# Layer 2's low-rank adapters folded into eight projection matrices while layer 1's experts run, with a reordered head and a pinned preparation of layer 3

## The chip, the cores and the metric

The kernel runs on one core of a Trainium2 chip. The metric is the device time of one execution in microseconds. TensorE (PE) does the matmuls and its weight loads are listed as PEld; VectorE is DVE, ScalarE is ACT, GpSimd is POOL, and SyncE (SP) issues most DMAs. Indirect DMAs (gathers by a list of indices) are issued by POOL. Everything is fp32.

## The reference, cut to what matters

Four layers run over a residual stream `x` of 32 sequences by 64 tokens by 512 values. Each layer is a conditioning step that depends on the sequence, followed by a feed-forward or attention block, and its result is added to `x`. Layer 0 is attention and seven experts, layer 1 is 32 experts with four chosen per token, layer 2 is a soft mixture of 16 experts, layer 3 is attention over a paged cache and a small product. The conditioning of layer 2 is what the change rewrites:

```python
def _L2_cond_ref(x, W, A, Bm, scalings, adapter_idx):
    N_ADAPTERS, RANK = (8, 16)
    H = jnp.einsum('btd,od->bto', x, W)
    A_b = A[adapter_idx]
    B_b = Bm[adapter_idx]
    s_b = scalings[adapter_idx]
    xa = jnp.einsum('btd,brd->btr', x, A_b)
    delta = jnp.einsum('btr,bor->bto', xa, B_b)
    delta = jax.lax.stop_gradient(delta * s_b[:, None, None])
    return H + delta
...
x = x + _L2_ffn_ref(_L2_cond_ref(x, L2_cond_W, ..., itok_B_0_6), ...)
```

So every sequence has one of eight adapters of rank 16, and its 64 tokens are multiplied by `W` transposed plus a low-rank product.

## The kernel before, in words

The 2048 rows of `x` are 16 tiles of 128 rows, and a tile holds two sequences. A matmul of the program is two instructions in the trace, since the values are fp32. A scheduler orders the instructions when the kernel is built; `g.pin` and `held` keep an operation in program order on its engine, `g.first` does so for the first matmul of a group, and a load marked `later` keeps its place.

The head (0 to about 366 us) loads constants, `x` and layer 0's weights on SP's queue in program order, gathers each sequence's 64x64 conditioning matrix (`wsel`) on POOL by an index `i_cond` that DVE computes from the conditions, and begins with the matmuls `mix`. Layer 0's experts follow to about 572 us. Beside them, once for each output tile, a generator called a `Side` puts in a piece of other work: `layer3_ahead` (line 2342) prepares index tables for layer 3's cache. Its operations on DVE are not pinned.

Layer 1 routes to about 690 us, and its experts run to about 1091 us. Their weights `wt` are gathered on POOL; the matmuls are `gu` (L1351), transposes `tp` (L1330) and `y` (L1364); DVE adds the bias `bd` into `yo`, four buffers, and SP writes it to the table `ys`. The `Side` here is `layer2_ahead` (line 1872), which loads layer 2's constants, makes a mask of adapters, and computes norms of layer 2's `mu` from 16 row blocks (`mus`).

Layer 2 takes about 1097 to 2045 us, 58.5 us a tile. For tile i it runs the soft mixture while it prepares tile i + 1: class `Lora` transposes the tile (`turn`, into `fT`), multiplies it with all eight adapters' A at once (`adapter`, L2110), masks the result by sequence on DVE (`am`, L2114), and multiplies with W and with B into one bank (`product`, L2122 and L2123). The layer normalisation after it goes over DVE (`st`, `ve`, `xl`), POOL (`rs`, gamma, beta, `nn`) and ACT. The residual of the tile after that comes from layer 1's table: `fetch` gathers four rows per token from `ys` (`yk`, three buffers) on POOL, and four pinned additions on DVE, add(0) to add(3), put them on `x`. The mixture's own order on TensorE in a tile is: dispatch (`ep`, `hp`), combine(0) to combine(3) (`gp`, L2311, one bank, emptied by DVE's `gT` copy, L2315) and project(0) to project(3) (`out`, L2320). POOL also gathers rows of layer 3's cache (`kvst`). In layer 2's start the load of `w2` (4 MB) goes out on ACT's queue.

Of the kernel before, what the change touches and what calls it, by code (L numbers as in the profile page):

```python
# [13 lines left out]
I32 = mybir.dt.int32  # L14
# [133 lines left out]
def _layout(i):  # L148
# [52 lines left out]
    a["w_2"] = _chunks(i["L2_cond_W"].T)  # L201
    a["w_a"] = _chunks(i["L2_cond_A"].reshape(P, D).T)
    a["w_b"] = i["L2_cond_Bm"].transpose(0, 2, 1).reshape(P, D)
# [49 lines left out]
class Prog:  # L253
# [96 lines left out]
    def per_half(self, pool, name):  # L350


        t = pool.tile([P, NT], I32, name=f"ih_{name}")
        for h in range(2):
            self.nc.sync.dma_start(
                out=t[64 * h : 64 * h + 64, :], in_=self.a[name][h].partition_broadcast(64)
            )
        f = pool.tile([P, NT], F32, name=f"fh_{name}")
        self.nc.vector.tensor_copy(f, t)
        return f  # L360

# [65 lines left out]
def layer0(g, w3, pool3):  # L427
    tc, nc, a = g.tc, g.nc, g.a
    with ExitStack() as ctx:
        keep = ctx.enter_context(tc.tile_pool(name="l0keep", bufs=1))  # L430
        g.constants(keep, "cst01")
        clear = g.results(keep)
        xs = g.stream("x0")
        ln2 = g.load(keep, "ln2")
        m = Moe(g, ctx, keep, E0, K0, [C0] * E0, V0, "w_e0", W0, l0_expert, ln2)
        with ExitStack() as c1:
            wp = c1.enter_context(tc.tile_pool(name="l0w", bufs=1))
            sb = c1.enter_context(tc.tile_pool(name="l0sb", bufs=2))
            at0 = g.cond_rows(wp, "cond0")
            x, other = {}, {}  # L440
# [12 lines left out]
            load(0)  # L453
            swapped(1)
            load(1)
            load(2)
            w = {k: g.load(wp, k) for k in ("ln1", "w_lat", "w_q", "w_kn", "w_kr", "w_v", "w_o", "w_r0")}
            shared = Shared(g)
# [524 lines left out]
def l1_expert(g, sb, hT, gate, up, bias, **kw):  # L983

    nc = g.nc
    ga = sb.tile([P, gate.shape[1]], F32, name="ga")
    nc.vector.tensor_scalar(ga, gate, bias[:, 0:1], 7.0, ALU.add, ALU.min)
    sg = sb.tile([P, gate.shape[1]], F32, name="sg", **kw)
    nc.scalar.activation(sg, ga, AF.Sigmoid, scale=1.702)  # L989
    up_ = sb.tile([P, gate.shape[1]], F32, name="up")  # L990
    nc.vector.tensor_scalar(up_, up, bias[:, 1:2], 7.0, ALU.add, ALU.min)
    nc.vector.tensor_scalar(up_, up_, -7.0, 1.0, ALU.max, ALU.add)
    g.pin(nc.gpsimd.tensor_tensor(ga, ga, sg, ALU.mult))  # L993
    nc.vector.tensor_tensor(hT, up_, ga, ALU.mult)


class Moe:
# [67 lines left out]
    def bias_of(self, e):  # L1065
        if self.bias and e < self.E and e not in self.bds:
            self.bds[e] = self.xp.tile([P, D], F32, name="bd", bufs=4)
            self.ask_bias(self.bds[e], e)
        return self.bds.get(e)
# [132 lines left out]
    def beyond(self):  # L1202
# [6 lines left out]
        with tc.If(n > 0), ExitStack() as ctx:  # L1209
# [67 lines left out]
            for t in range(V):  # L1277
                wt = sb.tile([P, self.wlen], F32, name="vwt", bufs=2)
                g.gather(wt, g.a[self.wname], widx[:, t : t + 1])
                xr = sb.tile([P, D], F32, name="vxr", bufs=1)  # L1280
                g.gather(xr, self.rows, stok[:, t : t + 1])
                xT = g.transpose4(ps, sb, xr, "vxT", self.scale)
                wg, wu, wd, bias = self.parts(wt)
                y = ffn(g, sb, ps, xT, wg, wu, wd, self.act, bias)
                yo = sb.tile([P, D], F32, name="vyo", bufs=2)
                if self.bias:
                    bd = sb.tile([P, D], F32, name="vbd", bufs=1)
                    g.gather(bd, g.a[self.bias], each[:, t : t + 1])
                    nc.vector.tensor_tensor(yo, y, bd, ALU.add)
                else:  # L1290
                    g.evac(yo, y)
                r = (self.tiles + t) * P
                nc.sync.dma_start(out=self.ys[r : r + P, :], in_=yo)
# [10 lines left out]
    def run(self, xs, per_tile):  # L1304
# [114 lines left out]
        def combined(pool, i, bufs):  # L1419
            x = g.load_x(pool, xs, i, bufs)  # L1420
            for k in range(K):
                kw = dict(name="yk", bufs=3) if k < 3 else dict(name="xl")
                yk = pool.tile([P, D], F32, **kw)
                g.gather(yk, self.ys, self.slot[:, i, k : k + 1], later=True)
                g.pin(nc.vector.scalar_tensor_tensor(x, yk, self.gates[:, i, k : k + 1], x, ALU.mult, ALU.add))
            return x

        def fetch(pool, i, bufs):
# [4 lines left out]
            def rows(k):  # L1433
                yk = pool.tile([P, D], F32, name="yk", bufs=3)
                g.gather(yk, self.ys, self.slot[:, i, k : k + 1], later=True)
                adds.append(partial(add, yk, k))
# [5 lines left out]

            for k in range(3):
                rows(k)
# [427 lines left out]
def layer2_ahead(g, w):  # L1872

    nc, a, first, pool = g.nc, g.a, w["first"], w["pool"]
    names = ("w_2", "w_a", "w_b", "mu", "w1")
    for k in names:
        w[k] = (pool if k in ("mu", "w1") else first).tile(list(a[k].shape), F32, name=f"sb_{k}", tag=f"sb_{k}")

    w["mask"] = pool.tile([P, B], F32, name="mask2")

    w["cmu"] = cmu = pool.tile([P, 16], F32, name="cmu")
    for k in names:
        for c in range(4 if k in ("mu", "w1") else 1):
            part = slice(None) if k not in ("mu", "w1") else (slice(None), slice(c, c + 1))
            g.dma(w[k][part], a[k][part])
            yield
    sb = w["sb"]
    scale = g.load_bcast(pool, "scale2")
    ad = g.load_bcast(pool, "adapt", I32)
    adf = pool.tile([P, B], F32, name="adf")  # L1890
    s8 = g.load(pool, "scal")
# [5 lines left out]
    nc.vector.tensor_copy(sc, sp)  # L1897
    nc.vector.tensor_scalar(w["mask"], adf, g.c("pd16"), sc, ALU.is_equal, ALU.mult)
    yield
    cs = pool.tile([P, 16], F32, name="cs2")  # L1900
    mus = {}
    for e in range(18):
# [6 lines left out]
        yield  # L1909
        if e < 16:  # L1910
            yield
    cn = g.power(pool, cs, "half", "cn")
    yield
    nc.vector.tensor_scalar(cn, cn, 1e-12, None, ALU.max)
    nc.vector.reciprocal(cmu, cn)
    nc.vector.tensor_scalar(cmu, cmu, scale, None, ALU.mult)


def layer2(g, w, combined, first, w3):
    tc, nc, a = g.tc, g.nc, g.a  # L1920
    with ExitStack() as ctx:
# [14 lines left out]
        x.append(t)  # L1936
        lora.adapter()
        yp = lora.product()
# [6 lines left out]
        next(norm)  # L1945
        lora.adapter()
        xn = next(norm)
# [11 lines left out]
        for i in range(NT + 1):  # L1959
# [31 lines left out]
            if early:  # L1991
                lora.turn()
                mix.sums()
                lora.adapter()
                soft.highest()
# [30 lines left out]
            if mix and not early:  # L2026
# [3 lines left out]
                mix.dispatch(0)  # L2030
                if lora:
                    lora.adapter()
                mix.turn(2)
                if lora:
                    norm = l2_norm_pieces(g, w, sb, s2, lora.product())
                    next(norm)
                    if i + 2 == NT:

                        w3["w_kv3"] = first.tile([P, 4, D], F32, name="w_kv3", tag="sb_w_2")
                        g.dma(w3["w_kv3"], a["w_kv3"])  # L2040
                        w3["x3"] = [first.tile([P, D], F32, name="x3", tag=f"sb_{k}") for k in ("w_a", "w_b")]
                        for j in range(2):
# [48 lines left out]
class Lora:  # L2091
# [12 lines left out]

    def adapter(self):

        g, nc, w, i = self.g, self.g.nc, self.w, self.i
        ap = self.ps.tile([P, 2, T], F32, name="ap2", tag="tp")
        for c in range(4):
            g.first(c, nc.tensor.matmul(  # L2110
                ap.rearrange("p b t -> p (b t)"), w["w_a"][:, c, :], self.xT[:, c, :], start=c == 0, stop=c == 3
            ))
        self.am = self.s2.tile([P, 2, T], F32, name="am")
        g.pin(nc.vector.tensor_tensor(  # L2114
            self.am, ap, w["mask"][:, 2 * i : 2 * i + 2].unsqueeze(2).to_broadcast([P, 2, T]), ALU.mult
        ))

    def product(self):
        g, nc, w = self.g, self.g.nc, self.w
        yp = self.ps.tile([P, D], F32, name="yp", tag="mm")  # L2120
        for c in range(4):
            g.first(c, nc.tensor.matmul(yp, self.xT[:, c, :], w["w_2"][:, c, :], start=c == 0, stop=False))  # L2122
        nc.tensor.matmul(yp, self.am.rearrange("p b t -> p (b t)"), w["w_b"], start=False, stop=True)  # L2123
        return yp

    def run(self):
        self.turn()
        self.adapter()
        return self.product()

# [211 lines left out]
def layer3_ahead(g, pool, w):  # L2342


    tc, nc, a = g.tc, g.nc, g.a
    w["kpos"] = pool.tile([P, B], F32, name="kpos")
# [7 lines left out]
    g.constants(sb, "cst3", later=True)  # L2354
    start = g.per_half(sb, "kvlen2")
    kvl = g.load_bcast(sb, "kvlen", I32)
# [5 lines left out]
    yield  # L2362

    w["ridx"] = ridx = sb.tile([P, NT], I32, name="ridx")
# [173 lines left out]
def layer3(g, w, xs, xb):  # L2538
# [3 lines left out]
    with ExitStack() as ctx:  # L2542
# [37 lines left out]
        with ExitStack() as c1:  # L2580
# [38 lines left out]
            for u in range(len(units) + 5):  # L2619
# [10 lines left out]
                if u < len(units):  # L2630
# [8 lines left out]
                    late = not z and i >= NT - LATE  # L2639
                    out = wp.tile([P, D], F32, name=f"qlate{i}") if late else sb.tile([P, D], F32, name="qkv3", bufs=6)  # L2640
                    outs.append(out)
# [310 lines left out]
```

## Time and profile before

| what | value |
| --- | --- |
| median of 3 runs | 2501.28 us (2495.75 to 2509.42) |
| profiled execution | 2500.39 us |
| its span | 2498.6 us |
| mean granted TensorE clock | 0.987 |
| PE busy | 2397.1 us, 96% |
| PEld busy | 1602.9 us, 64% |
| DVE busy | 1425.6 us, 57% |
| ACT busy | 716.1 us, 29% |
| POOL busy | 878.7 us, 35% |
| DMA moved | 341.46 MB, mean 137 GB/s |

The profiled execution is a single one, and the sums are made against its time. "Busy" counts an engine's instructions; several matmuls are in the pipeline at once, so a difference of start times is a better cost of a matmul than its duration. A row of a group names the line, the engine, the operation, the tile written and the tiles read, the shape, the count, then busy time in us and the mean ns of one, and last the idle time of the engine before these instructions and what ended it.

### The profile page before, as it was taken

To read this page: it belongs to the slowest core of one execution; us is meant where nothing else is said; L and a number is where in the kernel's file an instruction comes from. 1 tells how busy PE (TensorE), PEld (TensorE's weight loads), DVE (VectorE), ACT (ScalarE), POOL (GpSimd) and SP (SyncE) were. 2 spreads that over 40 slices of the span, in tenths; PEclk is the share of its full clock that TensorE was granted. 3 is DMA by queue.
4 is the path that set the end of the run, shared out by engine and by line. 5 is a ranking of instruction groups with operands and counts; after the bars stand their busy time and mean duration, and the time that the engine had idled before them with its cause. 6 is when DMAs were issued, how large, how long until landed. Compare 5 with 4: busy or idle time off the path is not lost.

```text
span 2498.6 us, 42594 instructions
## 1 busy us (share of the span) xinstructions
PE 2397.1 (96%) x16628; PEld 1602.9 (64%) x16643; DVE 1425.6 (57%) x3482; ACT 716.1 (29%) x1491; POOL 878.7 (35%) x923
## 2 busy tenths in 40 slices
PE   6999989999799999979999999999999999999998
PEld 4777766666566666747666666666666665446555
DVE  4667865835755545447445445554445441569887
ACT  2444521112311111102222222222222221246664
POOL 2122235604144434524333333333333221574440
PEclk9999999999799999989999999999999999999999
DMA  7242135537467977844222222222222223524441
GB/s 257 99 150 98 60 112 177 178 114 256 152 210 262 372 252 253 288 135 150 75 75 75 74 75 75 75 74 75 75 76 78 85 62 117 181 83 138 140 136 51
DMA packets 133560, 341.46 MB, mean 137 GB/s; under 512 B 24153, under 2 KB 25209, under 8 KB 126048
## 3 DMA queue, kind: packets, MB, share of 16 engines
q1 hardware_dynamic: 91184, 189.62, 22.0%
q0 software_dynamic: 41296, 142.68, 18.2%
q10 hardware_dynamic: 864, 6.29, 0.6%
q8 instruction: 135, 2.21, 0.4%
q14 instruction: 81, 0.66, 0.1%
HBM read 247.31 MB, written 107.22 MB: 142 GB/s over the span
## 4 chain that ended last, share of the span: by engine, by line
PE 50%; DVE 3%; issue 1%; POOL 1%; DMA 1%; ACT 1%; ACTq 0%; POOLq 0%; DVEq 0%
PE out L2320 9%; PE lp L2179 8%; PE zp L2256 8%; PE pp L2636 4%; PE hp L2288 3%; PE gp L2311 3%; PE yp L2122 2%; PE y L2887 2%; PE pT L2839 2%; PE sp L2817 2%; PE op L2865 2%; PE ep L2265 1%; PE kp L2790 1%; PE ap L2110 1%; PE out L2326 1%
## 5 line engine op out<-in xcount | busy, mean ns | idle before, releaser
L1351 PE MATMUL gu<-xT,wt 128*128 128x320 f32 (+5 forms) x1536 | 397.4, 406 | 6.6 <-DVE xT L1338 6.1
L1351 PEld LDWEIGHTS gu<-xT,wt 128*128 128x128 f32 x1536 | 283.1, 193 | 120.2 <-issue 48.6
L2179 PEld LDWEIGHTS lp<-xnT,sb_mu 128*128 128x128 f32 x2048 | 233.4, 192 | 10.8 <-issue 6.7
L2179 PE MATMUL lp<-xnT,sb_mu 128*128 128x128 f32 x2048 | 236.4, 275 | 3.6 <-DVE xnT L336 2.9
L2320 PE MATMUL out<-sb_w,gT 128*128 128x512 f32 x512 | 234.9, 602 | 0.0
L2256 PE MATMUL zp<-sb_w,xnT 128*128 128x512 f32 x512 | 226.7, 593 | 0.3 <-DVE z L2258 0.3
L1364 PE MATMUL y<-wt,hT 128*128 128x512 f32 (+2 forms) x544 | 199.9, 595 | 1.9 <-DVE yo L1372 1.3
L364 POOL DMA_INDIRECT kvst<-kv,gidx x96 | 92.9, 968 | 271.8 <-DMA oldkv<-kvst 201.9
L2256 PEld LDWEIGHTS zp<-sb_w,xnT 128*128 128x128 f32 x512 | 93.8, 190 | 105.3 <-issue 102.7
L2320 PEld LDWEIGHTS out<-sb_w,gT 128*128 128x128 f32 x512 | 92.2, 190 | 96.0 <-issue 92.8
L364 POOL DMA_INDIRECT yk<-ys,slot x95 | 98.9, 1041 | 124.7 <-SPq L1209 77.4
L2315 DVE COPY gT<-gp 128x512 f32<-128x512 f32 x64 | 44.3, 692 | 166.4 <-PE gp L2311 166.4
L364 POOL DMA_INDIRECT kvt<-newkv,oidxs x96 | 98.8, 1030 | 106.7 <-DMA kvt<-oldkv 54.4
L1364 PEld LDWEIGHTS y<-wt,hT 128*128 128x128 f32 (+2 forms) x544 | 72.8, 166 | 64.2 <-issue 50.7
L993 POOL TENSOR_TENSOR ga<-ga,sg 128x288 f32<-128x288 f32 (+5 forms) x66 | 50.8, 770 | 171.7 <-ACT sg L989 171.6
L364 POOL DMA_INDIRECT xr<-rows,stok x101 | 98.1, 971 | 34.7 <-issue 18.6
L2293 ACT ACTIVATE h<-hp 128x512 f32<-128x512 f32 x128 | 73.0, 596 | 119.3 <-PE hp L2288 105.8
L2267 ACT COPY ew<-ep 128x512 f32<-128x512 f32 x64 | 37.2, 583 | 198.6 <-PE ep L2265 198.6
L246 POOL TENSOR_TENSOR rstd<-ms,sb_cst 128x1 f32<-128x1 f32 x32 | 17.7, 552 | 213.5 <-DVE ms L246 213.5
L2217 POOL TENSOR_TENSOR eT<-eT,inv 128x512 f32<-128x512 f32 x64 | 67.0, 1049 | 70.1 <-DVE inv L2216 64.8
L2184 DVE TENSOR_TENSOR lT<-lp,cmu 128x512 f32<-128x512 f32 x64 | 44.1, 689 | 78.0 <-PE lp L2179 78.0
L2208 ACT ACTIVATE eT<-eT 128x512 f32<-128x512 f32 x64 | 40.3, 630 | 160.4 <-DVE eT L2205 160.2
(476 smaller groups left out, 4616.5 us busy)
## 6 DMA issues: line engine op xcount, KB each, us to landing
ys<-yo SPq DMA_DIRECT2D x106, 256.0 KB, 4.2
oldkv<-kvst SPq DMA_DIRECT2D x96, 224.0 KB, 2.2
kvt<-oldkv SPq DMA_DIRECT2D x96, 224.0 KB, 3.6
ys<-zero SPq DMA_DIRECT2D x10, 2048.0 KB, 12.1
xt<-x SPq DMA_DIRECT2D x59, 256.0 KB, 3.2
x<-xt SPq DMA_DIRECT2D x48, 256.0 KB, 2.0
wt<-w_e SPq DMA_DIRECT2D x7, 1536.0 KB, 6.9
sb_w<-w SPq DMA_DIRECT2D x5, 1024.0 KB, 13.9
```

Of the source, the lines that this page charges most:

```text
L364: ins = self.nc.gpsimd.indirect_dma_start(out=out, out_offset=None, in_=src, in_offset=bass.IndirectOffsetOnAxis(ap=idx, axis=0), **kw)
L993: g.pin(nc.gpsimd.tensor_tensor(ga, ga, sg, ALU.mult))
L1351: follow(nc.tensor.matmul(o, wj[:, c, ic * P : (ic + 1) * P], xTs[u][:, c, 0:n], start=c == 0, stop=c == 3))
L1364: follow(nc.tensor.matmul(y[row : row + n, :], hTs[e][:, ic, col : col + n], wd[:, ic, :], start=ic == 0, stop=ic == 1,))
L2179: g.first(e + c, nc.tensor.matmul(lp[:, e, :], w["mu"][:, c, (4 * q + e) * P : (4 * q + e + 1) * P], self.xnT[:, c, :], start=c == 0, stop ...
L2217: g.pin(nc.gpsimd.tensor_tensor(e3, e3, inv.unsqueeze(2).to_broadcast([P, 8, T]), ALU.mult))
L2256: g.first(c, nc.tensor.matmul(zp, self.xnT[:, c, :], w["w1"][:, c, cols], start=c == 0, stop=c == 3))
L2288: g.first(e + b, nc.tensor.matmul(hp[:, b, e, :], self.ews[q][r, e, :], self.z[q][r, e * P : (e + 1) * P], start=True, stop=True))
L2293: g.pin(nc.scalar.activation(self.hs[q][b], hp[:, b], AF.Gelu))
L2311: g.first(e + b + k, nc.tensor.matmul(gp[r, e, cols], self.hs[q][b][:, e, r], self.lT[q][:, e, cols], start=True, stop=True))
L2320: g.first(e, nc.tensor.matmul(self.out, self.gTs[q][:, e, :], w["w2"][:, 4 * q + e, :], start=False, stop=q + e == 6 and q == 3))
L2636: nc.tensor.matmul(pp, xT[i][:, c, :], (w["w_kv3"] if z else wq)[:, c, :], start=c == 0, stop=c == 3)
```

## The change

Layer 2's adapters are no longer applied to each tile. In layer 1's expert stage, 16 calls of `folded` compute, for each adapter and each quarter of the input dimension, the scaled product of A and B, add the quarter of W, and write the 128x512 block to a DRAM table `lora` of eight matrices of 1 MB. In a call two matmuls of 32 rows are in neighbouring row groups and go to the banks `tp` and `y`. In layer 2, two gathers per tile (one per sequence, 1 MB each) fetch the folded matrices, right after the product before; for tile 1 they go into the space of `w2`, whose load comes after. `product` now makes, for each quarter and each half of the tile (one sequence, 64 output columns of the array), one matmul with that sequence's matrix. `adapter` and its mask are gone.

To make room, `yk` has two buffers instead of three (in layer 1's last and layer 2's first tiles other space is used), `ga` and `up` two, `bd` three, `vwt` one. In the head, the constants `cst01` and the weights `ln2` are loaded later, the conditions earlier, and the first weights before the next tiles of `x`. In `layer3_ahead` DVE's operations are pinned in program order, and the first of them comes two pieces later. Two of layer 3's late tiles move into a half of the space of `x3`.

```diff
@@ head of layer 0
-        g.constants(keep, "cst01")
+        at0 = g.cond_rows(keep, "cond0")
         clear = g.results(keep)
         xs = g.stream("x0")
-        ln2 = g.load(keep, "ln2")
...
             load(0)
             swapped(1)
+            w = {k: g.load(wp, k) for k in ("ln1", "w_lat", "w_q", "w_kn", "w_kr")}
+            g.constants(keep, "cst01")
+            w["w_v"] = g.load(wp, "w_v")
             load(1)
             load(2)
-            w = {k: g.load(wp, k) for k in ("ln1", "w_lat", "w_q", "w_kn", "w_kr", "w_v", "w_o", "w_r0")}
+            ln2 = m.scale = g.load(keep, "ln2")
+            w.update({k: g.load(wp, k) for k in ("w_o", "w_r0")})
@@ fetch
             def rows(k):
-                yk = pool.tile([P, D], F32, name="yk", bufs=3)
+                kw = dict(name=f"z{k}") if i == 1 else dict(name="yk", bufs=2)
+                yk = pool.tile([P, D], F32, **kw)
                 g.gather(yk, self.ys, self.slot[:, i, k : k + 1], later=True)
                 adds.append(partial(add, yk, k))
...
-            for k in range(3):
+            for k in range(K if i == 1 else 2):
                 rows(k)
@@ layer2_ahead
+    def folded(c, v, k):
+        for j in (2 * k, 2 * k + 1):
+            bank = w["ps"].tile([P, D], F32, name="fold", tag=("tp", "y")[j % 2])
+            r = slice(32 * j, 32 * j + 32)
+            g.first(j % 2, nc.tensor.matmul(bank, scaled[v][r, c * P : (c + 1) * P], w_b[r, :], start=True, stop=True))
+            o = sb.tile([P, D], F32, name="fold", tag="yo", bufs=4)
+            nc.vector.tensor_tensor(o, bank, w_2[:, c, :], ALU.add)
+            e = 2 * j + v
+            g.dma(table[e * P : (e + 1) * P, c * D : (c + 1) * D], o)
...
         if e < 16:
+            folded(e // 4, e // 2 % 2, e % 2)
             yield
+    w["folded"] = {}
+    folded_rows(g, w, 0)
...
+def folded_rows(g, w, i, into=None):
+    for h in range(2):
+        t = into[h] if into else w["first"].tile([P, 4, D], F32, name=f"w_l{h}", tag=f"lora{h}")
+        g.gather(t.rearrange("p c d -> p (c d)"), w["lora"], w["lidx"][:, 2 * i + h : 2 * i + h + 1], later=True)
+        w["folded"].setdefault(i, []).append(t)
@@ layer2
-        lora.adapter()
+        second = wp.tile([P, 16, D], F32, name="w_l2", tag="sb_w2")
+        folded_rows(g, w, 1, (second[:, 0:4], second[:, 4:8]))
         yp = lora.product()
@@ Lora
     def product(self):
...
-            g.first(c, nc.tensor.matmul(yp, self.xT[:, c, :], w["w_2"][:, c, :], start=c == 0, stop=False))
-        nc.tensor.matmul(yp, self.am.rearrange("p b t -> p (b t)"), w["w_b"], start=False, stop=True)
+            for h in range(2):
+                r = slice(64 * h, 64 * h + 64)
+                g.first(c + h, nc.tensor.matmul(
+                    yp[r, :], self.xT[:, c, r], weights[h][:, c, :], start=c == 0, stop=c == 3
+                ))
+        if 0 < i < NT - 1:
+            folded_rows(g, w, i + 1)
@@ layer3_ahead
-    tc, nc, a = g.tc, g.nc, g.a
+    tc, a = g.tc, g.a
+    nc = SimpleNamespace(tensor=g.nc.tensor, vector=g.held.vector, sync=g.nc.sync)
...
-    start = g.per_half(sb, "kvlen2")
+    halves = g.halves(sb, "kvlen2")
...
     yield
+    yield
+    start = g.as_float(sb, "kvlen2", halves, nc.vector)
```

## The prediction

> **What bounds the kernel now.** I read the slices of the page first, then stretches by stage, then groups by shape, then the timeline of one stretch of each stage that is touched.
>
> ```profile
> PE 2397.1 (96%) x16628; PEld 1602.9 (64%) x16643; DVE 1425.6 (57%) x3482; ACT 716.1 (29%) x1491; POOL 878.7 (35%) x923
> PE   6999989999799999979999999999999999999998
> ```
>
> One slice is 62.5 us. TensorE is at 9 nearly everywhere but at the start, in slice 10 (layer 1's routing) and in slice 17 (the border of layers 1 and 2). By stage:
>
> ```profile
> 900.00:1060.00 160.00, 158.68 (x694) 111.24 (x693) 76.98 (x160) 27.39 (x71) 76.34 (x81) 1.00 0.78 266
> 1200.00:1400.00 200.00, 200.00 (x1507) 135.04 (x1507) 95.68 (x170) 49.60 (x80) 64.42 (x64) 1.00 0.25 75
> ```
>
> Columns: length, then PE, PEld, DVE, ACT, POOL busy, granted clock, DMA share, GB/s. Layer 2 (second row) has no idle TensorE, so a matmul taken from it is time taken from the kernel. Layer 1's experts (first row) lack only 1.3 us in 160, so a matmul put there is time added. The change moves TensorE work from one to the other; the forecast is that balance, plus what the new loads make late.
>
> **Layer 2's adapter goes.** One tile of 58.5 us, timeline of TensorE (start, duration):
>
> ```profile
> 1425.38 1.16 PE L2110 MATMUL ap<-fT,sb_w_a 128*128 128x128 f32 x8
> 1426.38 0.60 PE L2265 MATMUL ep<-sb_cst,eT 128*128 128x128 f32 x4
> 1426.82 3.60 PE L2122 MATMUL yp<-sb_w,fT 128*128 128x512 f32 x8
> 1430.25 1.02 PE L2123 MATMUL yp<-sb_w_b,am 128*128 128x512 f32 x2
> 1431.11 0.28 PE L2298 MATMUL dp<-sb_cst,csb 128*128 128x1 f32 x2
> ```
>
> Durations overlap through the pipeline, so I take start to start: `ap` 1426.38 − 1425.38 = 1.00, `yp<-am` 1431.11 − 1430.25 = 0.86. Together 1.86 us a tile; tiles 2 to 15 lie in the full stretch: 14 × 1.86 = **−26.0**. Tiles 0 and 1 belong to the border, below. The mask on DVE (0.29 us) goes too; DVE is half idle there, so nothing.
>
> **The product in halves.** A matmul of the program is two fp32 instructions. The 8 of `yp` become 16 of 64 output columns. They cost the same only if two column halves run together. Layer 1 has that form:
>
> ```profile
> 952.98 1.94 PE L1364 MATMUL y<-wt,hT 128*64 128x512 f32 x8
> 954.84 2.21 PE L1351 MATMUL gu<-xT,wt 128*128 128x288 f32 x8
> 956.89 1.88 PE L1364 MATMUL y<-wt,hT 128*128 128x512 f32 x4
> 958.60 3.83 PE L1351 MATMUL gu<-xT,wt 128*128 128x288 f32 x16
> ```
>
> Eight half-width instructions take 954.84 − 952.98 = 1.86 us, four full ones 958.60 − 956.89 = 1.71: halves do overlap, and a block of them costs 0.15 more. [...] I take the rows: product 14 × 0.15 = **+2.1**.
>
> **The fold in layer 1.** Sixteen calls, each of two program matmuls of 32 rows in neighbouring row groups, to two banks, 512 columns: four instructions of 0.43 us (1.71 / 4). Before has no such block at 512 columns; its row-split pairs are these:
>
> ```profile
> L2817 PE MATMUL sp<-kT,qT 64*128 64x336 f32 x256 | 55.1, 495 | 0.2 <-ACT kT L2794 0.2
> L2288 PE MATMUL hp<-z,ew 64*128 64x128 f32 x1024 | 74.4, 285 | 3.9 <-ACT h L2293 3.9
> ```
>
> 336 columns alone are 336/512 × 0.43 = 0.28 us, the row shows 55.1/256 = 0.215, which is 3/4; `hp` shows 73 ns where 107 would be alone, 2/3. So a pair takes about three slots of its four: my reading is that in a lone pair the second pass of the first can run beside the first pass of the second, and no more. 3 × 0.43 + 0.15 for the switch = 1.43, × 16 = **+22.9**. Ends: two slots, 16 × 1.0 = 16; four, 16 × 1.86 = 30.
>
> Beside it each call adds two DVE adds (an add of 128x512 out of a bank is 0.69 us), two SP writes of 256 KB and two `yo` buffers. DVE is 77 of 160 busy, and after `y` the trace has it waiting 1.2 us for the next `gu`. The writes are 8.4 MB in some 180 us, 47 GB/s on 266; slices go to 372. POOL isn't touched. Cover gone: an add before `up` delays `hT`, then `y`; hT to y is as short as 0.7 us. I take **+1** (0 to 10). The smaller rings (`ga`, `up`, `bd`) are in the same bound.
>
> **Gathers of the folded matrices.** Per tile two of 1 MB on POOL, right behind the product; the next product is 58 us later, so their landing is covered (in layer 1 a 1.5 MB gather lands in 8.4 us median, 12.4 at most). On POOL they hold back `rs`, gamma, beta, `nn`: two issues of about 1.3 us from 1429.5 push `rs` by about 1.4, but DVE's `gT` copy stood before `xl` in any case, so `xl` moves 0.5. Tile 0's two stand on POOL before the last expert's weights of layer 1 and hold that gather back 2.5 us; it is asked for more than an expert (about 12 us) ahead. Nothing on the path.
>
> **The later fetch of yk.** Two buffers instead of three: row k=2 is gathered after add(0), in POOL's order behind `nn`, and add(2) waits for it on DVE with `gT` behind it, whose bank combine(3) wants:
>
> ```profile
> 1440.08 1.02 POOL L364 DMA_INDIRECT yk<-ys,slot  x1 [0.18 <-issue]
> 1443.08 0.69 DVE L2315 COPY gT<-gp 128x512 f32<-128x512 f32 x1 [3.59 <-PE gp L2311]
> 1446.59 1.15 PE L2311 MATMUL gp<-lT,h 128*64 128x64 f32 x32
> ```
>
> The gather of k=2 takes the place of the first row: 1440.08 − 1.86 + 0.5 = 1438.7. Landing for `yk` in 1400 to 1900:
>
> ```profile
> DMA to landing us min/median/max: 3.4/3.7/4.7
> ```
>
> So 1442.4, add(2) to 1443.2, gT to 1443.9; combine(3) starts at 1444.7. Slack 0.8 us: **0**, but a landing over 4.5 us is paid by each tile. [...]
>
> **The border of layers 1 and 2.** Tile 1's matrices are gathered behind tile 1's row gathers (1107 or so), into the space of `w2`: they land about 1117, and product(1) waits for them as it waited before for `ap` and x (1118). The 4 MB load of `w2` and ACT's copies behind it wait for product(1). The two tiles' 3.7 us are lost again in that. **0** (−4 to +5).
>
> **Head and layer 3's preparation.**
>
> ```profile
> 13.08 1.97 PE L246 MATMUL mix<-xt,wsel 64*64 64x512 f32 x4 [13.08 <-DMA wsel<-wc,i_cond]
> 368.21 0.17 DVE L359 CAST fh_kvlen<-ih_kvlen 128x16 f32<-128x16 int32 x1 [2.47 <-DMA ih_kvlen<-kvlen]
> 370.59 0.18 DVE L2370 CAST kfc<-bc_kvlen 128x32 f32<-128x32 int32 x1 [1.73 <-DMA bc_kvlen<-kvlen]
> 371.24 2.29 PE L1351 MATMUL gu<-xT,wt 128*128 128x192 f32 x6 [4.83 <-DVE xT L1338]
> ```
>
> The first matmul waits for a gather by condition; two SP loads (0.95 us) move from before the conditions to behind: **−1** (−2.5 to +0.5). On SP the loads of x for tiles 1 and 2 now stand behind six weight loads and `cst01` (some 3 us); their first reader is tile 1's mix, behind tile 0's chain, and `ln2` is first read by the router. In layer 0's experts DVE stood in front of loads that had just been issued, and TensorE 4.83 us behind it. The cast comes two tiles later and DVE keeps program order: **−3.8** (about 1 of the 4.83 stays, as `xT` has its own work), and **+0.5** for bursts of small operations now in front of `xT`.
>
> **Sum**: −26.0 + 2.1 + 22.9 + 1 + 0 + 0 − 1 − 3.8 + 0.5 = −4.3, from the profiled 2500.39 to **2496**. That execution lies 0.9 us under the median, 2501.28. About 0.5%, 12.5 us, is what a measurement of this kernel can tell from no change.
>
> **The rivals.** (A) Slower: the third `yk` row comes late. Place: add(2) on DVE, then combine(3); it decides above a landing of 4.5 us. With the 2 MB at the slow end of layer 1's gathers, 12.4 us, they end at 1442 and `yk` lands at 1445 to 1446: 2 us a tile, 14 × 2 = 28, **2524**. For: one queue, 36 GB/s more. Against: this stage's DMA share is 0.25.
> (B) Faster: fold pairs overlap in two slots (−7), the border keeps its 3.7, the head and the preparation give their full 2.5: **2483**. For: `hp` at 2/3. Against: a lone pair has no successor to overlap with.
> (C) Layer 1 pays double: four slots (+7) and 0.8 us more in each call by DVE or DMA (+13): **2516**. Against: half-idle DVE.
> (D) Halves don't overlap, so the change does not do what it says: 16 × 3.4 = 55, **2551**. The `y` rows speak clearly against it.
>
> **How the numbers follow.** Main case 0.45 (own range 2487 to 2506), B 0.25, A 0.17, C 0.10, D 0.03. Faster by over 0.5% is under 2488: four fifths of B and 0.05 of the main case, 0.25. Slower is over 2513: most of A, half of C, all D, 0.22. Within: 0.53. The range leaves out the lower end of B and D with the greater part of A: 2480 to 2518.
>
> **What would show it.** Right: no `ap` and no `yp<-am`; `yp` 128*64 x16 near 3.6 us; a tile at 56.8 us with TensorE full; fold blocks of four instructions near 1.4 us; the layer-1 stage some 24 us longer and the wait at 371 gone. Wrong: waits of combine(3) for `gT` behind a `yk` landing (A), fold blocks of 1.0 (B) or 1.9 (C), `yp` near 7 us (D), or a border longer than 5 us more than before.

## The result: slower by half a per cent, and where it went

The changed kernel takes 2515.69 us (median of 8 runs, 2508.33 to 2521.24) beside 2501.78 us of the kernel before (8 runs): ratio 1.0055, 95% interval 1.0041 to 1.0068, some 14 us slower. A second group of runs, on its own chip, gave 1.0035 (1.0019 to 1.0051). The forecast was 2496 us in a range of 2480 to 2518: the time is inside, the sign is wrong.

Stages are compared by the start of the same matmul in two traces. The table gives how much longer each stage is than in the profiled execution of before (span 2498.6 us), for two profiled executions of the changed kernel (spans 2519.4 and 2511.4 us, the second from the second group). Beside it stand the prediction's terms.

| stage, and the matmul that ends it | forecast | first | second |
| --- | --- | --- | --- |
| head, layer 0, routing (last `y<-sb_w_shd,hT`) | −4.3 | −3.9 | −7.9 |
| layer 1's experts (last `y<-wt,hT`) | +23.9 | +35.5 | +30.9 |
| border, first tile of layer 2 (first `out<-sb_b,csb`) | −1.7 | +4.4 | +5.9 |
| rest of layer 2 (last `pp<-w_q,xT`) | −22.2 | −18.6 | −18.6 |
| layer 3 (last `y<-sb_w_o,oT`) | 0 | +2.0 | +1.2 |

Tile 2's product runs before the first `out`, so one of the fourteen tiles of the forecast, 1.7 of its 23.9 us, stands in the border's row. Three rows decide: layer 1 costs 7 to 12 us more than forecast, the border 6 to 8 more, and the rest of layer 2 gives 3.6 less. The 1 to 2 us of layer 3, and another 1.2 to 1.4 behind its last row, were not looked into.

The page of the changed kernel, busy times and then TensorE's slices:

```profile
PE 2411.0 (96%) x16660; PEld 1586.7 (63%) x16675; DVE 1443.9 (57%) x3504; ACT 717.6 (28%) x1491; POOL 906.0 (36%) x955
PE   7999989999799999987999999999999999999998
```

Two stretches of its trace, in the columns used before:

```profile
900.00:1060.00 160.00, 151.63 (x613) 95.54 (x611) 77.44 (x149) 23.31 (x59) 58.26 (x64) 0.96 0.75 259
1600.00:1800.00 200.00, 200.00 (x1528) 134.98 (x1527) 99.06 (x175) 51.11 (x82) 72.40 (x73) 1.00 0.35 111
```

Layer 2 is still full, as forecast. Layer 1's experts now lack 8.4 us of TensorE in 160 (1.3 before), and the clock in that stretch is 0.96 (1.00 before). What ended TensorE's waits there (us, times, longest):

```profile
PE fold L1923 <- ACT xT L334: 4.4, 3, 2.3
PE y L1372 <- DVE yo L1380: 2.9, 1, 2.9
PE fold L1923 <- DVE yo L1380: 1.1, 1, 1.1
```

Two of those waits in the timeline:

```profile
957.82 0.91 SPq L293 DMA_DIRECT2D mus<-mu_s  x1
966.30 0.63 ACT L1934 ACTIVATE mus<-mus 128x512 f32<-128x512 f32 x1 [10.11 <-DMA mus<-mu_s]
966.93 0.57 ACT L334 COPY xT<-tp 128x512 f32<-128x512 f32 x1
967.55 1.46 PE L1923 MATMUL fold<-sb_w_ab 32*128 32x512 f32 x4 [2.34 <-ACT xT L334]
...
1002.28 0.63 ACT L1934 ACTIVATE mus<-mus 128x512 f32<-128x512 f32 x1 [13.75 <-DMA mus<-mu_s]
1002.91 0.57 ACT L334 COPY xT<-tp 128x512 f32<-128x512 f32 x1
1003.52 1.12 PE L1923 MATMUL fold<-sb_w_ab 32*128 32x512 f32 x2 [0.93 <-ACT xT L334]
```

(Other instructions of these stretches are left out.) Read upward from the fold: it waits for a bank, the bank for ACT's copy of transposed rows, and that copy stands in ACT's order behind a sum of squares of layer 2's `mu` (`mus`), which had been put directly behind its own load and waited 10 to 14 us for it. Such waits were there before the change too, and cost TensorE 1.3 us in one place. ACT's waits in the stage, before and after:

```profile
ACT mus L1905 <- DMA mus<-mu_s: 98.1, 16, 9.3
```

```profile
ACT mus L1934 <- DMA mus<-mu_s: 84.7, 15, 13.8
```

The sum is no larger after (another 7.6 us of it are put down to `bd`); the longest has grown from 9.3 to 13.8. What a wait of ACT costs goes by what stands behind ACT at that moment, and not by its length alone: TensorE's 2.9 us for `yo` go back to a wait of ACT of only 7.05 us.

### The profile page after: what moved, and what is told of

Read it like the earlier page. It is cut to its first block, busy times and chain, and to the rows that moved or that the text cites. A ratio compares the mean times of both kernels' runs of the same rounds, so it can differ in the third digit from the quotient of the medians.

```text
span 2519.4 us, 42853 instructions
## 1 busy us (share of the span) xinstructions
PE 2411.0 (96%) x16660; PEld 1586.7 (63%) x16675; DVE 1443.9 (57%) x3504; ACT 717.6 (28%) x1491; POOL 906.0 (36%) x955
## 4 chain that ended last, share of the span: by engine, by line
PE 51%; DVE 2%; DMA 1%; POOL 1%; issue 1%; ACT 0%; ACTq 0%; POOLq 0%; DVEq 0%; SPq 0%
PE lp L2206 9%; PE out L2347 9%; PE zp L2283 8%; PE pp L2665 4%; PE hp L2315 3%; PE gp L2338 3%; PE yp L2151 2%; PE y L2916 2%; PE pT L2868 2%; PE sp L2846 2%; PE op L2894 2%; PE ep L2292 1%; PE kp L2819 1%; PE csum L2302 1%; PE out L2353 1%
## 5 line engine op out<-in xcount | busy, mean ns | idle before, releaser
L1359 PE MATMUL gu<-xT,wt 128*128 128x320 f32 (+5 forms) x1536 | 403.9, 411 | 4.3 <-DVE xT L1346 3.8
L370 POOL DMA_INDIRECT yk<-ys,slot x88 | 92.2, 1048 | 109.8 <-DVE pre L1465 68.2
L1380 DVE TENSOR_TENSOR yo<-y,bd 128x512 f32<-128x512 f32 (+3 forms) x88 | 60.7, 690 | 51.7 <-PE y L1372 46.6
```

What stands on the lines that cost most here:

```text
L370: ins = self.nc.gpsimd.indirect_dma_start(out=out, out_offset=None, in_=src, in_offset=bass.IndirectOffsetOnAxis(ap=idx, axis=0), **kw)
L1359: follow(nc.tensor.matmul(o, wj[:, c, ic * P : (ic + 1) * P], xTs[u][:, c, 0:n], start=c == 0, stop=c == 3))
L1380: nc.vector.tensor_tensor(yo[r], y[r], self.bds[e][r], ALU.add)
```

## The experiments

Each "stage" below is layer 1's experts, from the last `y<-sb_w_shd,hT` to the last `y<-wt,hT`; it is 443.1 us in the trace of before, 478.6 in the first trace after. It begins with some 34 us of routing; the waits given are those behind it. A stage is read from one trace, and the changed kernel's own differ by 5 us. Theory 1 was at first: the fold wants the bank `tp`, which ACT holds. Theory 2: the table's writes make loads land later. The first four ran on one chip, on which the kernel before took 2527.33 us, so only ratios and stages are compared with others.

**The sum of squares pinned**, two blocks behind its load.

```diff
-            nc.scalar.activation(m, m, AF.Square, accum_out=cs[:, e - 2 : e - 1])
+            g.pin(nc.scalar.activation(m, m, AF.Square, accum_out=cs[:, e - 2 : e - 1]))
```

> The changed kernel with one more pin: ACT's sum of squares of each mu block keeps its place in the program, two blocks after its load, instead of directly behind it. Theory 1 (ACT stands still on the block's load, the transposed rows' copy behind it holds the bank tp, and the fold wants that bank): the waits of the fold for ACT (4.4 us) and of y for yo (2.9) go, the clock stays at 1.00 between 940 and 1020 us, layer 1 ends about 12 to 14 us earlier, total about 2503. Theory 2 (the table's writes make everything land later): ACT still waits, the end of layer 1 moves by less than 3 us, total about 2514.

Stage 459.8 us, ratio 1.0034 (1.0016 to 1.0052). ACT no longer waits for `mus` at all, and of TensorE's waits in the stage one is left:

```profile
PE y L1372 <- DVE hT L1002: 0.6, 1, 0.6
```

The stage is 12.5 us shorter than the 472.3 of the full-width kernel below, which in this stage is the changed kernel. The total doesn't show it: in this trace a tile of layer 2 takes 60.46 us instead of 60.12, with some 0.3 us of `hp` waiting for ACT's `h` in each. The next two kernels show 60.46 as well, the fourth on the same chip does not. It isn't the pin: with it, on another chip, a tile takes 60.12 (below). The cause is left open.

**The fold's banks from the ring of gu.**

```diff
-            bank = w["ps"].tile([P, D], F32, name="fold", tag=("tp", "y")[j % 2])
+            bank = w["ps"].tile([P, D], F32, name="fold", tag="gu", bufs=4)
```

> The changed kernel with the fold's two banks taken from the ring of gu (four banks) instead of tp and y. Theory 1: the waits for ACT's copy go as in the pinned version, since the fold no longer needs tp; gu may wait some tenths for the adds, total about 2505. Theory 2: no change, about 2515.

Ratio 1.0039 (1.0017 to 1.0062), stage 471.3 us: 1 us less, which is nothing between single traces. The fold waits for nothing now, but `y` waits 2.4 us for `yo`, and `gu` 2.5 for what the trace calls issue. So the bank is only where the wait showed; theory 1 as put falls here.

**A table of W alone**: the writes stay, the fold's matmuls and additions go (it leaves out the adapters).

```diff
-            bank = w["ps"].tile([P, D], F32, name="fold", tag=("tp", "y")[j % 2])
...
-            g.dma(table[e * P : (e + 1) * P, c * D : (c + 1) * D], o)
+            g.dma(table[e * P : (e + 1) * P, c * D : (c + 1) * D], w_2[:, c, :])
```

> The changed kernel without the fold's matmuls and additions: the table gets W alone in all eight places, with the same writes (it leaves out the adapters). Theory 1: 16 folds at 1.25 us and the 14 us of stalls go, total about 2481. Theory 2 (stalls come from the writes): only the 20 us of matmuls go, total about 2496, and TensorE still waits for ACT.

Ratio 1.0016 (1.0005 to 1.0028), so neither number came out. The stage takes 456.0 us, still 12.9 over before, without a fold. `y` waits 7.2 us for `yo`, `gu` 2.6 for ACT's copy, and ACT 114.2 us for `mus`. Theory 2's half holds: the stalls come with the writes.

**Layer 2's product in full width**, the matrices alternating (it leaves out the adapter of one sequence for each quarter).

```diff
-            for h in range(2):
-                r = slice(64 * h, 64 * h + 64)
-                g.first(c + h, nc.tensor.matmul(
-                    yp[r, :], self.xT[:, c, r], weights[h][:, c, :], start=c == 0, stop=c == 3
-                ))
+            g.first(c, nc.tensor.matmul(yp, self.xT[:, c, :], weights[c % 2][:, c, :], start=c == 0, stop=c == 3))
```

> The changed kernel with layer 2's product in full width, eight instructions for a tile instead of sixteen halves, alternating between the two matrices (it leaves out the adapter of one sequence for each quarter). If the switch of tiling explains the 0.41 us that a tile's product costs over the old one, the tile period falls from 60.12 to 59.7 and the total by about 6, to 2509. If the halves cost only the 0.15 that was forecast and the rest is somewhere else, the period is about 59.97 and the total 2513.

A tile takes 59.77 us, 0.35 less than with halves. The timeline of the changed kernel first, then of this one:

```profile
1457.04 0.66 PE L2292 MATMUL ep<-sb_cst,eT 128*128 128x128 f32 x4
1457.63 3.65 PE L2151 MATMUL yp<-w_l,fT 128*64 128x512 f32 x16
1461.21 0.38 PE L2325 MATMUL dp<-sb_cst,csb 128*128 128x1 f32 x2
1461.53 1.16 PE L2315 MATMUL hp<-z,ew 64*128 64x128 f32 x16
```

```profile
1457.38 0.66 PE L2288 MATMUL ep<-sb_cst,eT 128*128 128x128 f32 x4
1457.88 3.60 PE L2149 MATMUL yp<-w_l,fT 128*128 128x512 f32 x8
1461.31 0.28 PE L2321 MATMUL dp<-sb_cst,csb 128*128 128x1 f32 x2
1461.52 1.16 PE L2311 MATMUL hp<-z,ew 64*128 64x128 f32 x16
```

Start to start, halves against full width: `ep` to `yp` 0.59 and 0.50, the block itself 3.58 and 3.43, `dp` to `hp` 0.32 and 0.21. The block costs the forecast 0.15; another 0.2 goes at its two neighbours (0.09 and 0.11). The total, 1.0058 (1.0038 to 1.0079), doesn't resolve 6 us here.

**The changed kernel again**, as the second group's yardstick.

> The changed kernel as it is, as the yardstick of this group on its chip: about 1.0055 times the kernel before, layer 1's experts about 29 to 35 us longer than before.

1.0035; its stages are in the table above. Stage 474.1 us.

**The writes alone, in the kernel before.**

```diff
+    table = g.dram.tile([8 * P, 4 * D], F32, name="lora")
...
+            for j in (2 * (e % 2), 2 * (e % 2) + 1):
+                at = 2 * j + e // 2 % 2
+                g.dma(table[at * P : (at + 1) * P, e // 4 * D : (e // 4 + 1) * D], w["w_2"][:, e // 4, :])
```

> The kernel before with the 32 writes of 256 KB in the places of the fold's writes, of W, to a table that nothing reads; nothing else is changed. If the writes make the blocks of mu land later and ACT, DVE and TensorE pass that on, layer 1's experts take 10 to 16 us more than before (443) and TensorE waits for yo or xT. If the stalls come from the smaller rings (ga, up, bd) or from the fold's banks, it is the kernel before within 3 us.

Ratio 1.0053 (1.0036 to 1.0071), stage 456.5 us: 32 DMA writes that no engine reads cost 13 us. The landings of `mus`, in the trace of before and in this one:

```profile
DMA to landing us min/median/max: 3.1/7.8/9.5
```

```profile
DMA to landing us min/median/max: 3.7/7.5/13.6
```

So not all the loads land later, only single ones. TensorE's waits:

```profile
PE y L1364 <- DVE yo L1372: 7.4, 1, 7.4
PE gu L1351 <- ACT xT L334: 2.6, 3, 2.0
```

The longest of them in this kernel's timeline:

```profile
966.26 0.39 SPq L293 DMA_DIRECT2D mus<-mu_s  x1
976.22 0.63 ACT L1906 ACTIVATE mus<-mus 128x512 f32<-128x512 f32 x1 [11.26 <-DMA mus<-mu_s]
977.31 0.41 ACT L989 ACTIVATE sg<-ga 128x256 f32<-128x256 f32 x1
977.81 0.72 POOL L993 TENSOR_TENSOR ga<-ga,sg 128x256 f32<-128x256 f32 x1 [8.32 <-ACT sg L989]
978.57 0.42 DVE L994 TENSOR_TENSOR hT<-up,ga 128x256 f32<-128x256 f32 x1 [10.22 <-POOL ga L993]
978.91 1.41 DVE L1372 TENSOR_TENSOR yo<-y,bd 96x512 f32<-96x512 f32 x2
980.46 3.75 PE L1364 MATMUL y<-wt,hT 128*128 128x512 f32 x4 [7.42 <-DVE yo L1372]
```

The load needs 10 us to land; ACT's gate `sg` waits behind the sum, POOL's product `ga` for the gate, DVE's `hT` and, in DVE's order, `yo` for that, and TensorE for `yo`.

**The smaller rings alone, in the kernel before** (`ga` and `up` two buffers, `bd` three).

```diff
-    ga = sb.tile([P, gate.shape[1]], F32, name="ga")
+    ga = sb.tile([P, gate.shape[1]], F32, name="ga", bufs=2)
...
-            self.bds[e] = self.xp.tile([P, D], F32, name="bd", bufs=4)
+            self.bds[e] = self.xp.tile([P, D], F32, name="bd", bufs=3)
```

> The kernel before with the smaller rings alone: ga and up two buffers, bd three. If the rings cause the stalls, layer 1's experts take 10 us or more longer; if the writes do, within 2 us of 443.

Ratio 1.0001 (0.9990 to 1.0012), stage 442.3 us. The rings cost nothing.

**The writes with the pin, in the kernel before**: the two edits above together.

> The kernel before with the 32 writes and with the pin of the mu sums. If the writes cost only by way of ACT standing on the blocks of mu, the 13 us of the version with writes alone go: layer 1's experts at 443 to 445 us, total as before. If they cost also by slower gathers of weights and rows, some of the 13 stays.

Ratio 0.9999 (0.9991 to 1.0008), stage 441.5 us. ACT's wait:

```profile
ACT mus L1906 <- DMA mus<-mu_s: 0.6, 1, 0.6
```

All 13 us are gone with the writes still made, though the stage now moves up to 347 GB/s in a stretch. So the bandwidth was there; the writes cost by way of one load and one in-order engine. The pin without the writes was not run, but it cannot be what hides the 13 us: behind the routing TensorE's waits add up to 2.7 us in the trace of before and to 1.4 in this one, and what the clock took (below) is 2.8 and 2.7.

This settles the cause of the writes' cost in layer 1: they make single loads of `mus` land later (13.6 us at most with the writes alone, 9.5 before; theory 2), and ACT's order passes it on to TensorE (what is left of theory 1).

**The pin, and the border's order**: tile 1's matrices are gathered before its rows, and add(2) and add(3) of the first fetch stand further back.

```diff
+        second = wp.tile([P, 16, D], F32, name="w_l2", tag="sb_w2")
+        folded_rows(g, w, 1, (second[:, 0:4], second[:, 4:8]))
         t, adds = combined.fetch(sb, 1, 4)
         x.append(t)
-        second = wp.tile([P, 16, D], F32, name="w_l2", tag="sb_w2")
-        folded_rows(g, w, 1, (second[:, 0:4], second[:, 4:8]))
...
-                if i == 0:
-                    add(2)
-                    add(3)
...
                     z.hidden(3)
                     next(rows, None)
+                if i == 0:
+                    add(2)
+                    add(3)
```

> The changed kernel with three edits: the pin of the mu sums, tile 1's matrices gathered before tile 1's rows instead of behind them, and add(2) and add(3) of the first fetch in the loop put behind the last hidden product. If the border's loss is those matrices standing behind the rows and DVE standing on late rows, TensorE's wait for w_l (3.3 us) and for xnT (5.0) fall to 1 and 3, and with the pin (12 us) the total is about 14 to 16 us under the changed kernel, even with the kernel before. If the border is bound by the bytes (4 MB before the second product in either order), only the pin's gain shows, and the pinned version's loss of 0.34 us a tile stays: 0.2 to 0.3% over the kernel before.

Ratio 1.0012 (1.0003 to 1.0021), 7 us better than the changed kernel in the same group. The stage is 461.9 us. In the border the wait for `w_l` is gone and the one for `xnT` falls from 5.0 to 1.7 us, but waits of 5.6 us for tile 1's rows and of 3.8 for DVE's `dg` are in their place. From the last `y<-wt,hT` to the first `out<-sb_b,csb` it is 102.0 us; the changed kernel has 101.8 and 103.3 in its two traces, before has 97.4. So the new order gains nothing that can be told from the spread. The bytes may be what is left (1 MB of rows for each of two tiles and 2 MB of matrices before the second product); that was not tried apart.

**Head and layer 3's preparation alone, in the kernel before.** The edit is the parts of the change that touch these two.

> The kernel before with the head's order and layer 3's preparation alone, nothing of layer 2. The traces of the changed kernel put layer 0's experts 5.8 us ahead of before and lose 2 to 3 of it at layer 0's end[...]; if that carries through, 2 to 4 us faster than before. If the saving is lost by the end of layer 1's routing, no change.

2496.86 beside 2501.52 us, ratio 0.9985 (0.9976 to 0.9994): these parts do pay, about 4 us.

**Four row groups in a call**, on top of the pin and the border's order: eight calls of four matmuls.

```diff
-        for j in (2 * k, 2 * k + 1):
-            bank = w["ps"].tile([P, D], F32, name="fold", tag=("tp", "y")[j % 2])
+        for j in range(4):
+            kw = dict(tag="gu", bufs=4) if j > 1 else dict(tag=("tp", "y")[j])
+            bank = w["ps"].tile([P, D], F32, name="fold", **kw)
...
-            folded(e // 4, e // 2 % 2, e % 2)
+            if e % 2 == 0:
+                folded(e // 4, e // 2 % 2, 0)
```

> The pinned version with the border's edits, and with the fold in eight calls of four matmuls in all four row groups (banks tp, y and two of gu) instead of sixteen calls of two. If matmuls in different row groups run fully side by side, as the pair's 1.06 us says, a call of four takes about 1.06 to 1.3 us as well, and layer 1's experts take 7 to 10 us less than in the version of sixteen pairs (462), total about 2495, under both kernels. If two is the limit, a call takes 2 us and nothing is gained; and the four buffers of yo, now filled in one burst, may hold DVE back by some us.

Ratio 1.0024 (1.0010 to 1.0038), stage 461.3 us, beside 461.9 with pairs: nothing gained, but the matmuls did what was hoped. The fold's group in the changed kernel, and here:

```profile
L1923 PE MATMUL fold<-sb_w_ab 32*128 32x512 f32 x64 | 20.4, 665 | 5.5 <-ACT xT L334 4.4 <-DVE yo L1380 1.1
```

```profile
L1925 PE MATMUL fold<-sb_w_ab 32*128 32x512 f32 x64 | 10.1, 640 | 0.0
```

DVE's wait here:

```profile
DVE fold L1929 <- DMA ys<-yo: 28.3, 11, 6.0
```

The same 64 instructions keep TensorE for half as long: a call of four takes the 1.07 us that a call of two took. The four sums want all four buffers of `yo` at once, DVE waits for their writes, and `gu` waits 6.9 us for its banks.

**Two of the four sums into dead space**, and first, on top of the four row groups.

```diff
-        for j, bank in enumerate(banks):
-            o = sb.tile([P, D], F32, name="fold", tag="yo", bufs=4)
+        for j in (3, 2, 0, 1):
+            bank = banks[j]
+            if j == 3:
+                o = w_a
+            elif j == 2 and c:
+                o = w_2[:, c - 1]
+            else:
+                o = sb.tile([P, D], F32, name="fold", tag="yo", bufs=4)
```

> The version with four row groups, with two of a call's four sums written into space that is dead by then (the unscaled A, and the quarter of W that is done) instead of into yo, and added first, since their banks are gu's. If DVE's 28 us of waiting for yo, and behind it TensorE's 6.9 us for gu, are what took the gain of four row groups, layer 1's experts take 452 to 455 us and the total is 4 to 7 us under the kernel before (0.997 to 0.9985). If not, it stays at 1.002.

2493.1 us beside 2501.37, ratio 0.9963 (0.9950 to 0.9976), stage 452.2 us. DVE's wait for the buffers, of the waits in the stage:

```profile
DVE fold L1935 <- DMA ys<-yo: 4.4, 3, 3.3
```

It was 28.3, and TensorE waits for nothing of the fold any more.

This version is 0.4% faster than the kernel before. The changed kernel was not run in this group; it stood at 1.0055 and 1.0035 in its own two.

## Why the prediction was wrong

The sum's frame held: TensorE bounds both stages, so what matters is the balance of what is put into layer 1 and taken from layer 2. Four terms were off.

The step that failed most, by enough to turn the sign of the sum alone, is "Beside it each call adds two DVE adds ... two SP writes of 256 KB ... I take +1 (0 to 10)". The cost of the writes was read from the bandwidth (47 GB/s on 266, slices to 372), and there was room, as the pinned writes show. It was not asked who waits for a single load. ACT did, 98 us in the trace of before, in plain sight in its waits; I passed over it since it cost next to nothing there. The writes alone measured +13. It is not the only step: with the pin the changed kernel is still at 1.0012.

Part of these 13 us is paid in TensorE's clock. Stretches of the changed kernel, the granted clock third from the end:

```profile
940.00:960.00 20.00, 20.00 (x83) 12.67 (x82) 11.30 (x22) 2.54 (x6) 8.41 (x10) 0.91 0.60 196
960.00:980.00 20.00, 17.66 (x73) 11.56 (x72) 8.05 (x16) 1.98 (x5) 6.64 (x7) 0.91 0.71 245
1000.00:1020.00 20.00, 18.01 (x58) 11.57 (x57) 7.63 (x16) 3.55 (x9) 6.00 (x7) 0.83 0.77 256
```

Granted clocks of 0.91, 0.91 and 0.83 over 20 us each are 7 us of full speed lost, by estimate, nearly as much again as the waits themselves. With the writes alone the sum closes: behind the routing, TensorE's waits rise from 2.7 to 11.4 us and the time lost to the clock (time times one minus the granted share) from 2.8 to 7.6, together 13.5, and that part of the stage is 13.1 us longer. The prediction's rival C (layer 1 pays double) had this outcome at 2516, half by luck: its +13 for DVE or DMA is the writes' size, but spread over the calls, and its +7 for serial matmuls was wrong.

The fold itself was sized too high, in the term 16 × 1.43 = 22.9. The "three slots" were taken from `hp` and `sp`; the call takes two slots (869.16 to 870.22, 1.06 us). Set against the same matmuls of before, those of the changed kernel fall behind by 1.25 us at each call where nothing waits, so a call costs 16 × 1.25 = 20. The two errors of this stage partly cancel.

In layer 2 the removal was right (1.86 us a tile), and the product's +0.15 was the mis-sized term. The tile, 61.57 us between starts of `out<-sb_b` before, is 60.12 after, 1.45 less: the halves cost 0.41. The forecast took one block's start-to-start out of layer 1 and left out the gaps at its neighbours. (The 58.5 us for a tile, in the prediction and ahead of it, were a misreading; the difference is what counts.) The 0.15 that the fold's sum has "for the switch" is that same block (1.86 beside 1.71 us). That a switch is what it pays for was the author's estimate; the runs show the 0.15 in the block and 0.2 at its neighbours, and not where they come from.

The border's 0 (−4 to +5) was missed: its row is 6.1 and 7.6 us over the forecast. Product(1) waits for its matrices, the load of `w2` for product(1), and ACT's copy behind that, in the changed kernel's timeline:

```profile
1147.02 1.04 PE L2151 MATMUL yp<-w_l,fT 128*64 128x512 f32 x2 [1.97 <-DMA w_l<-lora,lidx]
1154.62 0.33 ACTq L293 DMA_DIRECT2D sb_w<-w  x1
1156.41 0.59 ACT L334 COPY xnT<-tp 128x512 f32<-128x512 f32 x1 [7.36 <-DMA w_l<-lora,lidx]
1157.05 14.56 PE L2206 MATMUL lp<-xnT,sb_mu 128*128 128x128 f32 x128 [1.88 <-ACT xnT L334]
```

These places were named; their price was set at nothing. The longest wait behind them was not. The same block in the kernel before, then in the changed kernel with what DVE stood on:

```profile
1157.47 3.84 PE L2179 MATMUL lp<-xnT,sb_mu 128*128 128x128 f32 x32 [2.95 <-DVE xnT L336]
```

```profile
1184.85 0.75 DVE L1447 SCALAR_TENSOR_TENSOR xt<-yk,gates,xt 128x512 f32<-128x512 f32 x1 [2.15 <-DMA yk<-ys,slot]
1187.01 0.75 DVE L1447 SCALAR_TENSOR_TENSOR xt<-yk,gates,xt 128x512 f32<-128x512 f32 x1 [1.41 <-DMA yk<-ys,slot]
1192.13 6.10 PE L2206 MATMUL lp<-xnT,sb_mu 128*128 128x128 f32 x32 [5.01 <-DVE xnT L336]
```

With two buffers the third row of `yk` is gathered late, which is rival A's mechanism. DVE stands 3.6 us on such rows (1.6 before), TensorE waits 2.1 us longer, and the block takes 2.3 us more at a granted clock of 0.60. These two are as large as the border's loss in this trace. That they are its cause is argued from the order of these lines and not shown by a run.

Right were, behind the border: the matrices' landing (9.0 us at most) is covered in every later tile; `yk` comes as late as worked out and costs next to nothing. Its landing, of the tile's answer, from 1230 to 2060 us:

```profile
DMA to landing us min/median/max: 3.4/3.6/5.5
```

The one tile where it shows, in the timeline:

```profile
1472.56 1.02 POOL L370 DMA_INDIRECT yk<-ys,slot  x1 [2.81 <-issue]
1476.12 0.75 DVE L1447 SCALAR_TENSOR_TENSOR xt<-yk,gates,xt 128x512 f32<-128x512 f32 x1 [7.21 <-DMA yk<-ys,slot]
1477.62 1.15 PE L2338 MATMUL gp<-lT,h 128*64 128x64 f32 x32 [0.75 <-DVE nn L2186]
```

DVE stands for 7.2 us and combine(3) waits 0.75; in 1600 to 2000 us TensorE has no idle time at all. So rival A was real in its mechanism, and in these tiles there was just enough slack.

The head gave 3.4 us at its first matmul (13.08 to 9.66), of which 1.8 were left at the first `op` (49.59 to 47.76); 1 was forecast. Much of this is spread: with the old head the first matmul starts at 9.82 to 11.71 us in the traces of three experiments (the writes, the rings, the writes with the pin). Layer 3's preparation gave 2.3 us in the first trace (layer 0's marks go from −3.5 to −5.8) and 6.2 in the second (−3.5 to −9.7); 3.8 was forecast. The wait for `xT` that was to go is still 3.05 us in the first trace, at 373.75, and 0.86 in the second: the pinned DVE now stands in front of its operation on `bc_qs`, 6.97 us in the first and 4.78 in the second. In both, 1.9 us is lost again at layer 0's end, where the wait before the next stage is 3.05 us in the first trace instead of 2.19 and the same block then runs slower, 7.22 us instead of 5.60 in the trace of before (but see the last section). The changed kernel's timeline:

```profile
567.73 7.22 PE L246 MATMUL gu<-hnT,sb_w_sh 128*128 128x128 f32 x48 [3.05 <-PEq L1217]
```

## What to carry to other kernels

Before adding DMA traffic to a full stage, list the engines that wait for a load in order, even those whose waits cost nothing, and see what stands behind each in that engine's order: mean bandwidth doesn't tell what a later landing will cost (13 us here, in a stage that moved 347 GB/s in a stretch), and the length of the wait alone doesn't either (98 us of ACT's waits cost TensorE 1.3 us before, and a single one of 7.05 us cost it 2.9 after). A load's consumer that an in-order engine meets right behind its issue is worth pinning further back before anything else is tuned (with the writes it took 1.0053 to 0.9999). Price a change of the array's tiling by the time from the instruction before the block to the one after it, in the place where it will stand. Before a gain of 2 us in one trace is put down to a change, look at the same place in a second trace.

## What the runs showed of the hardware that was not expected

Matmuls of 32 rows in different row groups ran fully side by side: from the fold's start to that of the next instruction it is 1.06 us for two and 1.07 for four.

The granted clock fell behind short waits, but the length of the wait did not decide it. The block at layer 0's end in the writes with the pin, then with four row groups:

```profile
571.01 7.22 PE L246 MATMUL gu<-hnT,sb_w_sh 128*128 128x128 f32 x48 [2.04 <-DVEq L1209]
```

```profile
564.09 5.59 PE L246 MATMUL gu<-hnT,sb_w_sh 128*128 128x128 f32 x48 [3.12 <-PEq L1217]
```

Behind the wait of 2.04 us the granted clock was 0.50 for 3.4 us, behind that of 3.12 it stayed at 1.00. So the slow block of the changed kernel (0.50 for 3.4 us, behind a wait of 3.05) is not shown to come of its longer wait, which is how the expectation for the head and layer 3's preparation alone puts it; in the trace of before the clock stayed at 1.00 behind 2.19 us. What decides was not looked into.

The same kernel took 2501 us on some chips and 2527 on another, 1% apart, twice the size of the effect that was studied. In the four traces from that other chip layer 3 (as in the table) takes 286 to 287 us, in the rest 268 to 271; why stays open.
